# An attention and mixture-of-experts layer on one core: unread products, another order of the row products and earlier projections in its opening

## The chip, the cores and the metric

The kernel runs on one NeuronCore of a Trainium2 chip. A core has TensorE (PE: matrix products into PSUM, with weight loads, PEld, beside them), VectorE (DVE), ScalarE (ACT), GpSimd (POOL) and SyncE (SP), which mainly issues DMAs; each works through its own instructions in order. The metric is the time of one execution on the device in microseconds, and lower is better. A profiled execution also leaves a trace, whose span runs from the first to the last instruction.

## The reference, cut to what matters

The input x is 8 sequences of 1024 tokens of 256 numbers. Attention has 16 heads of 16; keys and values are the same rotated projection. Then 8 experts each take the 1024 tokens that score highest for them.

```python
x = x + attn(layernorm(x), Wq, Wkv, Wout, bout)
x = x + moe(layernorm(x), gate_w, ln_w, ln_b, fc1s, b1s, fc2s, b2s)

def attn(x, ...):
    q, kv = split(x @ Wq), split(x @ Wkv)            # 16 heads of 16
    q, kv = rotary(q) * 16 ** -0.5, rotary(kv)
    out = softmax(q @ kv.T) @ kv
    return merge(out) @ Wout + bout

def moe(x, ...):                                      # x: 8192 tokens
    scores = softmax(x @ gate_w.T)
    w, idx = top_k(scores.T, 1024)                    # for each of 8 experts
    y = layernorm(x[idx]) * ln_w + ln_b
    out = (gelu(y @ fc1.T + b1) @ fc2.T + b2) * w
    return x.at[idx].add(out)
```

## The kernel before

**Tiling and stages.** All tiles have 128 rows. Attention goes batch by batch (8) and, in a batch, over 4 groups of 4 heads. A group has 16 steps: for the row maxima a step is one tile of 128 queries against half of the keys; for the exponentials it is 128 keys against half of the queries. The maxima run 13 steps ahead of the exponentials (`LEAD`), so the main loop starts at step -13, and the first exponentials come at step 0. Then the experts' tokens are selected, gathered and put through the two layers.

**Numbers in two halves.** [...] So q, k and the differences of neighbouring keys ("steps", tile `s`) are cut into a high half `hi` and the rest `lo`, and one product over 64 rows (16 dimensions times four combinations of halves) gives an exact score. `split_halves` makes hi and lo for q and k, `split_steps` (L361) for the key differences (`dhi`, `dlo`). The halves are written to DRAM (`q_d`, `k_d`, `s_d`) in the laid-out order and loaded back as `q`, `k` and `s`. For the first heads the trip through DRAM would take long, so `rows_at_once` (L164) lays hi and lo out on TensorE: a product with `picks` copies rows of hi and lo to their places, two pairs of heads beside each other, and ACT or DVE copies the result into the `q` and `k` tiles.

**A step.** `row_max` makes a score product `ps_x` (L536), which VectorE reduces to a row maximum (L543); there are four in a step. `score_pass` makes `ps_s` (L587) from `s` and `q` with a last product that takes the maximum away (from the tile `top`, which `lay_max` sends through DRAM, L573 and L577), ACT takes the exponential (L620), and `weigh_values` multiplies with the values (`ps_av`, L639).

**PSUM.** `ps_m` has four buffers of one bank and serves nearly everything: `ps_x`, transposes `ps_t`, `ps_av`. `ps_e` has two of two banks, for `ps_s`, the row products `ps_r`, and the projections `ps_p` of heads 8 to 15 in the first batch. A buffer can be written again once its last reader is done.

**What sets the order.** The order on each engine is the order in which the program emits instructions. The rest of the work is cut into pieces by generators: each `yield` ends a piece and names its kind ("x" is heavy and comes one to a step, in step -1 and before in every step, later in every second). `run_pieces` advances up to two of the tasks in `starts` by one piece, after the step's own score products. The first of them is `prologue(0)`: it normalises and turns x, projects heads 0 to 7 (`c` = 0), rotates them (`rotate`, on VectorE at first, later on POOL), transposes and splits them with four calls of `rows_at_once`, and goes on with heads 8 to 15 (`c` = 1): 8 projections, one for each tile of 128 tokens (L292), then four transposes with their splits. Up to the point where `ready[0, 0]` is set the pieces are run at once, before step -13; the last `rows_at_once` comes in step -13, the two `split_steps` of heads 0 to 7 in steps -12 and -11, and the projections in steps -10 to -3. Writes wait in `pending` until `issue_pending` hands them to SP, whose queue then holds in order: the writes of q and k, the loads of the next group's k and q, the late weights, the writes of `s_d`, the loads of `s`.

Of the kernel before, what the change touches and what calls it, by code (L numbers as in the profile page):

```python
# [8 lines left out]
F32 = mybir.dt.float32  # L9
# [10 lines left out]
P = 128  # L20
H = 16
DH = 16
# [5 lines left out]
def preln_attention_moe_kernel(  # L28
# [18 lines left out]
    nc = tc.nc  # L47
# [11 lines left out]
    QW = 512  # L59
# [18 lines left out]
    same = const.tile([P, P], F16, name="same")  # L78
# [19 lines left out]
    with ExitStack() as actx:  # L98
# [62 lines left out]
        picks = prob.tile([P, 4, P], F32R, tag="e", name="picks")  # L161
        nc.gpsimd.tensor_copy(picks, picks_f)

        def rows_at_once(hi, lo, keys, dst, eng):  # L164

            pt = ps_e.tile([P, 2, QW], F32, tag="e", name="ps_r")
            for pair in range(2):
                dims = slice(2 * DH * pair, 2 * DH * (pair + 1))
                for part, half in enumerate((hi, lo)):
                    nc.tensor.matmul(  # L170
                        pt[:, pair],
                        lhsT=picks[dims, 2 * keys + part],
                        rhs=half[dims],
                        start=(part == 0),
                        stop=(part == 1),
                    )
            if eng is nc.scalar:
                nc.scalar.copy(dst, pt)
            else:
                nc.vector.tensor_copy(dst, pt)  # L180
# [102 lines left out]
        def project(b, t, xnT, qk, c, n):  # L283

            if b == 0 and c > 0:

                pp = ps_e.tile([P, 2, QW], F32, tag="e", name="ps_p")[:, 0, 0 : 2 * n * P]
            else:
                pp = ps_m.tile([P, QW], F32, tag="m", name="ps_p")[:, 0 : 2 * n * P]
            for kc in range(DC):  # L290
                w = wqkv[:, kc, :, c * P : (c + n) * P]
                nc.tensor.matmul(  # L292
                    pp,
                    lhsT=xnT[:, kc, t % T2 * P : (t % T2 + 1) * P],
                    rhs=w.rearrange("p a d -> p (a d)") if n == DC else w,
                    start=(kc == 0),
                    stop=(kc == DC - 1),
                )
            rotate(b, t, pp, qk, c, n)
# [4 lines left out]
        def issue_pending():  # L304
            while pending:
                fn, *args = pending.pop(0)
                fn(*args)
# [53 lines left out]
        def split_steps(b, hf, c, full):  # L361


            dif = side.tile([P, QW], F32, tag="u", name="dif")
            if hf == 0:
                nc.gpsimd.tensor_copy(dif[:, 0:P], full[:, 0:P])
                tails[0] = small.tile([P, P], F32, tag="tail", name="tail", bufs=1)
                nc.gpsimd.tensor_copy(tails[0], full[:, QW - P : QW])
            else:
                nc.gpsimd.tensor_tensor(dif[:, 0:P], full[:, 0:P], tails[0], ALU.subtract)  # L370
            nc.gpsimd.tensor_tensor(dif[:, P:QW], full[:, P:QW], full[:, 0 : QW - P], ALU.subtract)
            hi = side.tile([P, QW], F32R, tag="hi", name="dhi")
            lo = side.tile([P, QW], F32R, tag="lo", name="dlo")
            (nc.scalar.copy if b == 0 and c == 0 else nc.gpsimd.tensor_copy)(hi, dif)
            nc.gpsimd.tensor_tensor(lo, dif, hi.bitcast(F32), ALU.subtract)
            rows, cols = slice(c * P, (c + 1) * P), slice(hf * QW, (hf + 1) * QW)
            pending.append((write_halves, halves[b][2], rows, cols, hi, lo, True))
            if hf == 1:
                pending.append((steps_ready.setdefault, (b, c), True))
# [8 lines left out]
        def prologue(b):  # L388

            q_d = dram.tile([2, D, 4, QW], F32, tag="q_d", name=f"q_d{b}", bufs=2)  # L390
            k_d = dram.tile([D, 4, N], F32, tag="k_d", name=f"k_d{b}", bufs=2)
            s_d = dram.tile([D, 4, N], F32, tag="s_d", name=f"s_d{b}", bufs=2)
            halves[b] = (q_d, k_d, s_d)
            if b == 0:
                k = kq.tile([P, 2, N], F32R, tag="k", name="k_0", bufs=2)
                grp[0] = {
                    "k": k,
                    "q": [
                        kq.tile([P, 2, QW], F32R, tag="q", name=f"q_0_{hf}", bufs=4)
                        for hf in range(2)  # L400
                    ],
                }
                xts = [xt_first, load_x(b, 1)]
            else:
                xts = [load_x(b, hf) for hf in range(2)]
                yield 6 if b == 1 else 2
            qks = []

            def normalised(hf):
                stats = yield from row_stats(xts[hf], "a", 2 if b == 0 else 1)  # L410
                scaled(nc.vector if b == 0 else nc.gpsimd, xts[hf], xts[hf], stats)

            def turned(hf):

                tag = "aoT" if b == 0 and hf == 1 else "T"
                xnT = one.tile([P, DC, QW], F32, tag=tag, name=f"xnT_{b}_{hf}")
                for c in range(DC):
                    pt = transposed(lambda t: xts[hf][:, t, c * P : (c + 1) * P])
                    nc.scalar.copy(xnT[:, c, :], pt)
                qks.append(side.tile([P, T2, 2, D], F32, tag="qk", name=f"qk_{b}_{hf}"))  # L420
                return xnT

            if b == 0:

                xnTs = []
                yield from normalised(0)
                yield "x"
                xnTs.append(turned(0))
                yield from normalised(1)
                for hf in range(2):  # L430
                    if hf == 1:
                        yield "x"
                        xnTs.append(turned(1))
                    for j in range(T2):
                        yield "x"
                        project(b, T2 * hf + j, xnTs[hf], qks[hf][:, j], 0, 1)
            else:
                yield from normalised(0)
                yield from normalised(1)
                yield 3  # L440
                for hf in range(2):
                    yield "x"
                    xnT = turned(hf)
                    if hf == 0:


                        yield (2 * T * NG * (b - 1) - 5,)
                    for j in range(T2):
                        yield "x"
                        project(b, T2 * hf + j, xnT, qks[hf][:, j], 0, DC)  # L450
            for c in range(DC):
                fulls = []
                if b == 0 and c > 0:
                    for t in range(T):
                        yield "x"
                        project(b, t, xnTs[t // T2], qks[t // T2][:, t % T2], c, 1)
                if b == 0 and c == 0:

                    for n, (hf, s) in enumerate(((0, 0), (0, 1), (1, 1), (1, 0))):
                        yield "x"  # L460
                        pt = transposed(lambda j: qks[hf][:, j, s, 0:P])
                        full = split_halves(b, hf, c, s, pt)
                        if s == 1:
                            fulls.append((full, pt))
                        issue_pending()
                        if n > 0:
                            rows_at_once(*at_once.pop(0))
                    for n, (full, pt) in enumerate(fulls):
                        nc.scalar.copy(full, pt)
                        fulls[n] = full  # L470
                    ready[b, c] = True

                    yield "s"
                    rows_at_once(*at_once.pop(0))
                else:
                    for hf in range(2):
                        for s in range(2):
                            yield "x"
                            issue_pending()
                            pt = transposed(lambda j: qks[hf][:, j, s, c * P : (c + 1) * P])  # L480
                            full = split_halves(b, hf, c, s, pt)
                        yield 2
                        issue_pending()
                        split_steps(b, hf, c, full)
                if b == 0 and c == 0:
                    for hf in range(2):
                        yield "s"
                        split_steps(b, hf, c, fulls[hf])
                        issue_pending()
            yield 2  # L490
            issue_pending()

# [989 lines left out]
```

## Time and profile before

| | |
|---|---|
| median of 3 runs | 2214.38 us (2210.72 to 2216.36) |
| profiled execution | 2207.54 us |
| span of its trace | 2205.8 us |
| mean granted TensorE clock | 0.978 of full |
| PE busy over the span | 2056.1 us (93%) |
| DVE busy over the span | 1765.4 us (80%) |
| opening, to the first row maximum | 29.6 us |
| step 0, first product for exponentials | 61.6 us |

Lines of the profile give a start and a length in microseconds, the engine, the line of the kernel, the operation, output and inputs by the program's names, and the count of instructions that a row sums up. A bracket at the end says how long the engine had been idle before and what ended the wait. "Busy" counts an instruction from its start to its end; products overlap, so a row of eight is shorter than eight single ones.

### The profile page before, as it was taken

Reading aid. Unit: us, or ns where it says so; the run is one execution under the profiler, and the core shown is the slowest. Engines: PE = TensorE matmul, PEld = TensorE weight load, DVE = VectorE, ACT = ScalarE, POOL = GpSimd, SP = SyncE. Lnnn points to the kernel's source line nnn. Section 1 sums busy time; section 2 is a strip of 40 time slices with the busy share of each in tenths; the row PEclk is TensorE's granted clock in tenths of the full one; section 3 lists DMA queues with packets and bytes.
Section 4 is the critical chain, followed back from the end, with each engine's and each line's share of the span. In section 5 each row is a group of like instructions: output and inputs, shape, how many; then the busy total and the mean of one; then the engine's idle time right before and its main releaser. Section 6 shows DMA issues by size and latency. Waiting matters only on the chain.

```text
span 2205.8 us, 35134 instructions
## 1 busy us (share of the span) xinstructions
PE 2056.1 (93%) x12528; PEld 1100.0 (50%) x12528; DVE 1765.4 (80%) x3446; ACT 1384.7 (63%) x1791; POOL 1272.5 (58%) x1320
## 2 busy tenths in 40 slices
PE   7999999999999999999999999999993599999998
PEld 4444544444444444444444444444431376666665
DVE  8988888998998899889989988989946646666654
ACT  2777777777887777878777877877781112222222
POOL 6667585848485766758584867644242144444442
PEclk9999999999999999999999999999996699999999
DMA  6523624632372356236323722552114033333322
GB/s 178 191 88 123 238 81 147 223 122 78 136 257 73 104 202 206 96 107 225 143 78 143 270 67 102 188 208 88 41 41 135 20 75 75 77 77 77 76 42 24
DMA packets 152703, 271.53 MB, mean 123 GB/s; under 512 B 15056, under 2 KB 67664, under 8 KB 152400
## 3 DMA queue, kind: packets, MB, share of 16 engines
q1 hardware_dynamic: 139088, 250.62, 32.9%
q0 software_dynamic: 12288, 17.05, 4.7%
q8 instruction: 99, 1.62, 0.3%
q10 hardware_dynamic: 1152, 1.62, 0.2%
q14 instruction: 76, 0.62, 0.1%
HBM read 143.93 MB, written 125.04 MB: 122 GB/s over the span
## 4 chain that ended last, share of the span: by engine, by line
PE 71%; DVE 16%; issue 4%; POOL 3%; ACT 2%; DMA 2%; POOLq 0%; ACTq 0%; SPq 0%; DVEq 0%
PE ps_av L639 20%; DVE mx L543 14%; PE ps_x L536 13%; PE ps_o L1333 10%; PE ps L1279 8%; PE ps_s L587 7%; PE ps_p L292 5%; PE ps_t L251 3%; PE ps_o L727 3%; PE ps_h L1238 1%; POOL xf L242 1%; ACT e L620 1%; PE ps_d L665 1%; DVE xr L735 1%; PE ps_y L1194 1%
## 5 line engine op out<-in xcount | busy, mean ns | idle before, releaser
L543 DVE TENSOR_REDUCE mx<-ps_x 128x1 f32<-128x512 f32 x2048 | 1264.1, 681 | 153.1 <-PE ps_x L536 139.8
L620 ACT ACTIVATE e<-ps_s 128x1024 f32<-128x1024 f32 x1024 | 995.4, 1025 | 88.6 <-PE ps_x L536 42.1
L536 PE MATMUL ps_x<-k,q 64*128 64x512 f32 x2048 | 718.9, 449 | 19.7 <-DVE mx L543 6.2
L587 PE MATMUL ps_s<-q,s 64*128 64x512 f32 x2048 | 622.2, 428 | 9.0 <-ACT e L620 6.1
L536 PEld LDWEIGHTS ps_x<-k,q 64*128 64x128 f32 x2048 | 347.4, 185 | 414.1 <-DVE mx L543 287.8
L639 PE MATMUL ps_av<-e,v 128*32 128x512 f32 x4096 | 492.5, 598 | 6.9 <-DVE mx L543 0.9
L654 POOL TENSOR_TENSOR av<-av,avp 128x512 f32<-128x512 f32 x190 | 242.4, 1276 | 396.4 <-ACT avp L652 380.2
L587 PEld LDWEIGHTS ps_s<-q,s 64*128 64x128 f32 x2048 | 314.0, 185 | 46.9 <-ACT e L620 29.6
L1333 PE MATMUL ps_o<-w,hT 128*128 128x256 f32 x1024 | 230.2, 381 | 0.0
L639 PEld LDWEIGHTS ps_av<-e,v 128*32 128x32 f32 x4096 | 107.0, 109 | 241.7 <-issue 163.6
L1343 POOL DMA_INDIRECT out<-o,idx x64 | 103.0, 1609 | 212.9 <-DVE o L1342 80.2
L1333 PEld LDWEIGHTS ps_o<-w,hT 128*128 128x128 f32 x1024 | 191.8, 190 | 29.3 <-issue 4.8
L652 ACT COPY avp<-ps_av 128x512 f32<-128x512 f32 x192 | 112.8, 587 | 144.4 <-PE ps_av L639 139.9
L1231 ACT ACTIVATE hT<-mid,b 128x512 f32<-128x512 f32 x112 | 77.9, 719 | 98.9 <-DVE mid L1306 73.9
L1291 ACT COPY mid<-ps 128x512 f32<-128x512 f32 x28 | 16.0, 571 | 195.7 <-PE ps L1279 195.7
L292 PE MATMUL ps_p<-wqkv,xnT 128*128 128x512 f32 (+1 forms) x288 | 129.8, 578 | 4.5 <-DVE mx L543 4.1
L1341 DVE TENSOR_TENSOR o<-ps_o,b2b 128x256 f32<-128x256 f32 x64 | 27.1, 423 | 128.8 <-PE ps_o L1333 126.2
L269 POOL TENSOR_TENSOR u<-pe,sin 128x256 f32<-128x256 f32 (+1 forms) x128 | 86.2, 695 | 53.8 <-ACT pe L263 53.8
L1179 POOL DMA_INDIRECT g<-rows_d,idx x64 | 63.9, 998 | 92.1 <-issue 68.0
L339 POOL CAST hi<-full 128x512 fp32r<-128x512 f32 x60 | 36.9, 615 | 89.8 <-ACT full L337 80.7
L273 POOL TENSOR_TENSOR qk<-pe,u 128x512 f32<-128x512 f32 (+1 forms) x72 | 83.3, 1157 | 7.2 <-DVE pe L271 2.2
L340 POOL TENSOR_TENSOR lo<-full,hi 128x512 fp32r<-128x512 f32 x60 | 76.9, 1281 | 7.5 <-DMA s_d<-dlo 2.9
(200 smaller groups left out, 2323.8 us busy)
## 6 DMA issues: line engine op xcount, KB each, us to landing
s<-s_d SPq DMA_DIRECT2D x64, 512.0 KB
k<-k_d SPq DMA_DIRECT2D x62, 512.0 KB
q<-q_d SPq DMA_DIRECT2D x124, 256.0 KB
s_d<-dhi SPq DMA_DIRECT2D x32, 512.0 KB
s_d<-dlo SPq DMA_DIRECT2D x32, 512.0 KB
w<-in_fc_t SPq DMA_DIRECT2D x16, 1024.0 KB
q_d<-hi SPq DMA_DIRECT2D x30, 512.0 KB
q_d<-lo SPq DMA_DIRECT2D x30, 512.0 KB
```

Source lines behind the costliest of these rows:

```text
L269: eng.tensor_tensor(u[:, :, a * hd : (a + 1) * hd], v4[:, :, 1 - a, :], s3, ALU.mult)
L292: nc.tensor.matmul(pp, lhsT=xnT[:, kc, t % T2 * P : (t % T2 + 1) * P], rhs=w.rearrange("p a d -> p (a d)") if n == DC else w, start=(kc == 0),
L536: nc.tensor.matmul(pt, lhsT=q[r : r + 64, h // 2, j * P : (j + 1) * P], rhs=k[r : r + 64, h // 2, kh * QW : (kh + 1) * QW], start=True, st ...
L543: nc.vector.tensor_reduce(grp[i]["mx"][:, kh, h, j : j + 1], pt, AX.X, ALU.max)
L587: nc.tensor.matmul(pt[:, h % 2, :], lhsT=ones_r[r : r + 64, :] if last else k[r : r + 64, pair, kt * P : (kt + 1) * P], rhs=(top_bufs[half ...
L620: nc.scalar.activation(e.rearrange("p h q -> p (h q)"), pt.rearrange("p h q -> p (h q)"), AF.Exp, scale=DH**-0.5,)
L639: nc.tensor.matmul(pa[HS * h : HS * (h + 1), :], lhsT=v_bufs[b % 2][:, kt, c : c + HS], rhs=es[h // 2][:, h % 2, :], start=(n == 0), stop= ...
L652: nc.scalar.copy(part, pa)
L654: (nc.vector if end else nc.gpsimd).tensor_tensor(av, av, part, ALU.add)
L1279: nc.tensor.matmul(ph, lhsT=lhsT, rhs=rhs, start=True, stop=True)
L1333: nc.tensor.matmul(po, lhsT=h[:, f, j * P : (j + 1) * P], rhs=weights[e][1][:, f, :], start=(n == 0), stop=(n == FC - 1),)
L1343: nc.gpsimd.indirect_dma_start(out=out_rows[:, :], out_offset=bass.IndirectOffsetOnAxis(ap=idx[:, t : t + 1], axis=0), in_=o, in_offset=No ...
```

## The change

A helper `busy(n)` emits n products of the 128x128 matrix `same` with itself, read four times over, into a `ps_m` buffer that nobody reads. `rows_at_once` takes the high halves of both pairs first and then both low halves, with one such product ahead of each; it is called four times. Two more stand after the point where `ready[0, 0]` is set. The two `split_steps` of heads 0 to 7 lose their own pieces and go into those of the first two projections of heads 8 to 15, so that the projections begin in step -12 rather than -10, and everything that `prologue(0)` does after them comes two steps sooner.

```diff
+        def busy(n):
+
+            for _ in range(n):
+                pb = ps_m.tile([P, QW], F32, tag="m", name="ps_b")
+                nc.tensor.matmul(
+                    pb.rearrange("p (a q) -> p a q", a=4),
+                    lhsT=same,
+                    rhs=same.unsqueeze(1).to_broadcast([P, 4, P]),
+                    start=True,
+                    stop=True,
+                )
+
         def rows_at_once(hi, lo, keys, dst, eng):
 
             pt = ps_e.tile([P, 2, QW], F32, tag="e", name="ps_r")
-            for pair in range(2):
-                dims = slice(2 * DH * pair, 2 * DH * (pair + 1))
-                for part, half in enumerate((hi, lo)):
+            for part, half in enumerate((hi, lo)):
+                busy(1)
+                for pair in range(2):
+                    dims = slice(2 * DH * pair, 2 * DH * (pair + 1))
                     nc.tensor.matmul(
                         pt[:, pair],
                         lhsT=picks[dims, 2 * keys + part],
                         rhs=half[dims],
...
                 if b == 0 and c > 0:
                     for t in range(T):
                         yield "x"
+                        if t < 2:
+                            split_steps(b, t, 0, first_fulls[t])
+                            issue_pending()
                         project(b, t, xnTs[t // T2], qks[t // T2][:, t % T2], c, 1)
...
                     ready[b, c] = True
+                    busy(2)
 
                     yield "s"
                     rows_at_once(*at_once.pop(0))
...
                 if b == 0 and c == 0:
-                    for hf in range(2):
-                        yield "s"
-                        split_steps(b, hf, c, fulls[hf])
-                        issue_pending()
+                    first_fulls = fulls
             yield 2
             issue_pending()
```

## The prediction

> **What bounds the kernel now.** I read the page first: how busy each engine is, and the TensorE clock over the span.
>
> ```profile
> PE 2056.1 (93%) x12528; PEld 1100.0 (50%) x12528; DVE 1765.4 (80%) x3446; ACT 1384.7 (63%) x1791; POOL 1272.5 (58%) x1320
> PE   7999999999999999999999999999993599999998
> PEclk9999999999999999999999999999996699999999
> ```
>
> TensorE bounds the whole, but a slice is 55 us wide and the edit lives in the first 70. So I asked for windows of the opening, cut where the granted clock changes.
>
> ```profile
> 24.86:28.28 3.42, 3.33 (x18) 1.91 (x19) 1.66 (x3) 2.09 (x3) 1.00 (x3) 1.00 0.80 174
> 28.28:31.69 3.41, 2.80 (x13) 1.18 (x11) 3.41 (x6) 2.12 (x4) 1.41 (x3) 1.00 0.92 199
> 31.69:35.10 3.41, 3.41 (x8) 1.46 (x6) 3.41 (x7) 1.40 (x2) 2.00 (x4) 0.51 0.93 204
> 35.10:38.52 3.42, 3.42 (x7) 1.90 (x7) 3.42 (x6) 0.62 (x1) 1.97 (x2) 0.50 0.85 258
> 38.52:41.95 3.43, 3.43 (x10) 1.86 (x10) 2.21 (x5) 0.37 (x1) 1.59 (x3) 0.50 1.01 353
> 58.90:62.30 3.40, 3.04 (x17) 1.63 (x15) 3.40 (x7) 1.18 (x3) 3.15 (x6) 1.00 0.25 71
> ```
>
> Columns: length, busy time and count of PE, weight loads, DVE, ACT, POOL, then clock, DMA share, GB/s. From 31.7 to 42.0 us TensorE runs at half clock. But from 28.3 on the full column is DVE's: 3.41 of 3.41, except in one window (2.21). VectorE's own timeline says what that exception is.
>
> ```profile
> 28.94 0.68 DVE L333 TENSOR_TENSOR lo<-ps_t,hi 128x512 fp32r<-128x512 f32 x1
> 29.61 9.68 DVE L543 TENSOR_REDUCE mx<-ps_x 128x1 f32<-128x512 f32 x16
> 40.50 9.74 DVE L543 TENSOR_REDUCE mx<-ps_x 128x1 f32<-128x512 f32 x16 [1.22 <-PE ps_x L536]
> ```
>
> The row maxima run back to back at 9.68/16 = 0.605 us each; between 29.6 and 62 us VectorE waits once, 1.22 us, for TensorE. It stays at 47.2 of 48.4 us to 110 us, and only then TensorE takes over (88.0 of 90 us). So a microsecond here is worth one at the end only if it moves the VectorE row of maxima: its start (29.61), or its one hole.
>
> TensorE's timeline gives both.
>
> ```profile
> 25.56 0.66 PE L251 MATMUL ps_t<-ident,qk 128*128 128x128 f32 x4
> 26.15 0.74 PE L170 MATMUL ps_r<-kl,picks 32*128 32x512 f32 x4
> 26.82 0.66 PE L251 MATMUL ps_t<-ident,qk 128*128 128x128 f32 x4
> 27.40 1.28 PE L170 MATMUL ps_r<-kl,picks 32*128 32x512 f32 x4
> 29.08 1.77 PE L536 MATMUL ps_x<-k,q 64*128 64x512 f32 x4 [0.40 <-DVE k L180]
> ...
> 37.67 2.07 PE L292 MATMUL ps_p<-wqkv,xnT 128*128 128x256 f32 x4
> 43.47 1.13 PE L292 MATMUL ps_p<-wqkv,xnT 128*128 128x256 f32 x4
> ```
>
> The first score product waits for the copy of k (VectorE, 27.81 to 29.02). The hole is the first projection at half clock: 2.07 us against 1.13. VectorE had at most four products in PSUM, 4 x 0.605 = 2.4 us; the projection plus the next product's 0.6 us is more.
>
> **The change, part by part.** *Unread products.* Ten: two in each of four `rows_at_once`, two before step -13. The experts' opening has the same product:
>
> ```profile
> 1740.39 1.90 PE L1088 MATMUL ps_b<-ones_h,same 128*128 128x512 f16 x8
> ```
>
> One alone takes 0.38 us at full clock, so seven steps take 1.90 - 0.38: 0.217 us each, 2.2 us in all. Nobody reads them; they cost where TensorE had no gap. Those of the first call go into waits for hi (23.76 to 24.00) and lo (24.5 to 24.9). From 25.56 on TensorE is nearly full. Summing starts: transposes 25.56 + 0.59; k's first rows 0.67 + two products 0.43, so the next transposes stand at 27.25, k's second rows at 27.84. There product, hi, product bring the lo pair to about 28.5 (its lo is ready at 27.89, no wait now) and its end to 28.75; two more give 29.2 against 29.08: +0.1 us. If each also pays its weight load (0.10 us in the experts' rows), six make +0.7. A buffer can add as much: the four PSUM buffers of that pool are held here by transposes awaiting later readers, and a product put into the last one waits for lo (end 29.62), so scores start near 29.85, +0.75. Below nothing: 0.1 us, through hi pairs now side by side. I take +0.4 us, between the sum of starts and the ends, range -0.1 to +0.75.
>
> *High before low.* Same products, same durations; both hi products of a call can go before lo arrives. It is counted in the -0.1.
>
> *The clock.* [...] I go by the trace: clock held, hole gone, -1.22 us. Ends: 0 and -1.22.
>
> *Projections two steps sooner.* Two empty stops vanish; both `split_steps` stay at steps -12 and -11, now each ahead of a projection, and all later work for heads 8 to 15 moves two steps (4.8 us) up. On TensorE 8 projections x 1.13 = 9.0 us stand in steps that VectorE fills with 2.42 us against 0.9 + 1.13 of TensorE: hidden. If the dip comes all the same, they help: the first projection goes out after the eighth score product, 32.4 to 34.5, the window to 35.1 is then as full as the one that ended the dip, and the hole is about 0.6 instead of 1.22.
>
> POOL: a projection costs it 0.87 + 0.73 + 0.73 + 0.29, every 2.79 us by its starts (43.01, 45.80, 48.60), more than a step. The second `split_steps` now queues behind the first rotation: POOL is done with the first dlo at 34.4, rotates to 37.2 (37.6 at half clock), differences 1.5, ACT's copy 0.6, dlo 1.3: 40.7 to 41.1 instead of 37.8. Who waits is SP:
>
> ```profile
> 42.71 1.19 SPq L315 DMA_DIRECT2D s_d<-dlo  x1
> ```
>
> ```profile
> 58.36 1.49 SPq L577 DMA_DIRECT2D top<-top_d x2
> 61.93 0.62 PE L587 MATMUL ps_s<-top,ones_r 64*128 64x512 f32 x2
> ```
>
> SP reaches that write only at 42.7, behind the loads of k, q and the late weights, so 1.6 us of cover remain; gone, each further microsecond delays s, then top_d, which queues behind s. The top load issued at 58.36 won't come sooner, while its product would be due at 61.1; a wait there of up to 0.8 us is hidden, because VectorE is then still 1.1 us behind (max 53 starts at 29.61 + 52 x 0.605 + 1.22 + 0.42 = 62.7). PE's backpressure through two copies and two PSUM tiles reaches four projections back: the eighth, at 50, needs the fourth rotation, done at 49. Cover 1 us, price 0.4 us a projection. SP's writes for heads 8 to 15 come after the top loads in its order and find DMA at 0.25: 0. ACT issues the same copies: 0. After step 9 every queue's order is as before.
>
> **Sum**: +0.4 - 1.22 + 0 = -0.8 us. The profiled execution took 2207.54 us (span 2205.8), so 2206.7; it lies 6.8 below the runs' median 2214.38, to which I apply the same difference: **2213.6 us**.
>
> **Rivals.** (a) *It does not do what it says*: the dip comes all the same. +0.4 - 0.6 = -0.2, at worst with a buffer wait +0.75 - 0: **2214.2 to 2215.1**. [...] (b) *Faster by more*. The chain that ended last has places where it waits for DMA:
>
> ```profile
> 216.99 4.90 DMA q<-q_d
> ```
>
> There the second batch's queries come late, and near 437 the score products wait 2.1 us for top. If the shifted opening lets both transfers win, -0.8 - 4.8 - 2.1 = -7.7: **2206.7**. For it: such waits stand at some batch boundaries and not at others (none at 640, 1030). Against: the order after step 9 is unchanged, so issue and need shift together. (c) *Slower*: the late dlo. If POOL's rotation holds the second dlo past 42.7 + 1.6 us of slack at top, about 44.3, every microsecond more delays the exponentials of step 0 and, with TensorE in order, the maxima. From 51.7 on it outweighs the 0.8 by 6.6; at 52.8 it is 8.5 - 0.8 = 7.7: **2222**. It needs over ten microseconds beyond my 41, for instance through ACT's in-order copies waiting on POOL. (d) A boundary stall added, the opposite of (b): +4.9 or so, **2219**.
>
> **How the numbers follow.** Forecast 0.5; (a) 0.24; (b) 0.11; (c) 0.09; (d) 0.06. A difference within 0.3%, 6.6 us, is about what a measurement of this kernel can tell from no change (three runs of it span 5.6 us). Forecast, (a) and half of (d) are within it: same 0.77; faster 0.11; slower 0.12. The range: forecast to (d), plus the runs' own 2.8 us to either side, cut where (b) and (c) begin: 2209 to 2219.
>
> **What the changed profile would show.** Right: clock 1.00 from 31.7 to 42; the maxima start at 29.9 to 30.3 with no hole to step 0; first projection of heads 8 to 15 near 33; s_d<-dlo still issued near 42.7. Wrong: a first score product later than 30.4; a hole of a microsecond with clock 0.5; SP waiting for POOL dlo; top late with VectorE idle; or all this as said and the end elsewhere, at the DMA waits of the batch boundaries.

## The result: slower by 0.19%

| | before | changed |
|---|---|---|
| median | 2213.22 us (12 runs) | 2216.7 us (12 runs) |
| ratio, 95% interval | 1 | 1.0019 (1.001 to 1.0028) |
| span of the profiled execution | 2205.8 us | 2213.2 us |
| mean granted TensorE clock | 0.978 | 0.977 |

The change costs 4.2 us, 2.2 to 6.2 by the interval, where 0.8 us of gain was forecast. The page of the changed kernel (busy time of each engine, and the clock over 40 slices of the span) looks as before.

```profile
PE 2060.6 (93%) x12538; PEld 1101.1 (50%) x12538; DVE 1767.1 (80%) x3446; ACT 1384.2 (63%) x1791; POOL 1270.5 (57%) x1320
PEclk9999999999999999999999999999996699999999
```

The ten products more are there, and no slice of 55 us shows a difference. The windows of the opening do (length, busy time and count of PE, PEld, DVE, ACT, POOL, clock, DMA share, GB/s).

```profile
28.28:31.69 3.41, 3.07 (x11) 1.08 (x11) 2.21 (x4) 2.30 (x4) 0.72 (x3) 1.00 0.92 198
31.69:35.10 3.41, 3.41 (x12) 1.25 (x11) 1.78 (x4) 1.11 (x2) 0.76 (x1) 0.60 0.93 204
35.10:38.52 3.42, 3.42 (x9) 1.94 (x10) 2.74 (x6) 0.79 (x2) 2.13 (x3) 0.50 0.87 277
38.52:41.95 3.43, 3.43 (x14) 1.91 (x13) 3.43 (x7) 0.14 (x1) 3.11 (x5) 0.90 0.97 337
```

VectorE, which was full here in every window but one, is busy 2.21, 1.78 and 2.74. TensorE looks fuller, yet its clock still goes to half, at 32.3 instead of 31.7, and comes back at 39.1 instead of 42.0. VectorE's timeline names the holes.

```profile
28.70 0.68 DVE L346 TENSOR_TENSOR lo<-ps_t,hi 128x512 fp32r<-128x512 f32 x1
30.59 2.49 DVE L557 TENSOR_REDUCE mx<-ps_x 128x1 f32<-128x512 f32 x4 [1.20 <-PE ps_x L550]
34.70 2.48 DVE L557 TENSOR_REDUCE mx<-ps_x 128x1 f32<-128x512 f32 x4 [1.63 <-PE ps_x L550]
37.86 14.44 DVE L557 TENSOR_REDUCE mx<-ps_x 128x1 f32<-128x512 f32 x24 [0.68 <-PE ps_x L550]
...
55.69 16.97 DVE L557 TENSOR_REDUCE mx<-ps_x 128x1 f32<-128x512 f32 x28 [0.46 <-PE ps_x L550]
```

Before, the maxima started at 29.61 and had one hole of 1.22. Now they start 0.98 later, and the holes are 1.63, 0.68 and 0.46. Sum: 0.98 + 2.77 - 1.22 = +2.5 us; the rest lies in waits too short for the rows to name. As a mark I use the start of the second layout of the maxima (the row `parts<-mx`), called the opening's end: 69.94 before, 72.70 now, +2.76. TensorE's timeline shows what stands in front of the maxima.

```profile
25.32 0.66 PE L264 MATMUL ps_t<-ident,qk 128*128 128x128 f32 x4
25.82 0.38 PE L168 MATMUL ps_b<-same 128*128 128x512 f16 x1
26.12 0.50 PE L183 MATMUL ps_r<-kl,picks 32*128 32x512 f32 x2
26.56 0.39 PE L168 MATMUL ps_b<-same 128*128 128x512 f16 x1
26.88 0.50 PE L183 MATMUL ps_r<-kl,picks 32*128 32x512 f32 x2
27.31 0.65 PE L264 MATMUL ps_t<-ident,qk 128*128 128x128 f32 x4
...
29.30 0.82 PE L168 MATMUL ps_b<-same 128*128 128x512 f16 x2
30.05 0.62 PE L550 MATMUL ps_x<-k,q 64*128 64x512 f32 x2
...
32.61 0.61 PE L168 MATMUL ps_b<-same 128*128 128x512 f16 x1
33.15 0.79 PE L183 MATMUL ps_r<-lo,picks 32*128 32x512 f32 x2
33.87 1.22 PE L550 MATMUL ps_x<-k,q 64*128 64x512 f32 x4
...
55.16 0.73 PE L550 MATMUL ps_x<-k,q 64*128 64x512 f32 x4 [0.51 <-ACT mrows L585]
```

The first score product goes out at 30.05 instead of 29.08, behind the products. The last row products and their two unread ones (31.77 to 33.87) stand between the scores of steps -13 and -12 and meet the half clock: that is the hole of 1.63. The score products at 55.16 wait for ACT's copy of the row maxima (`mrows`): that is the hole of 0.46.

### The profile page after: what moved, and what is told of

Read it like the earlier page. It is cut to its first block, busy times and chain, and to the rows that moved or that the text cites. A ratio compares the mean times of both kernels' runs of the same rounds, so it can differ in the third digit from the quotient of the medians.

```text
span 2213.2 us, 35158 instructions
## 1 busy us (share of the span) xinstructions
PE 2060.6 (93%) x12538; PEld 1101.1 (50%) x12538; DVE 1767.1 (80%) x3446; ACT 1384.2 (63%) x1791; POOL 1270.5 (57%) x1320
## 4 chain that ended last, share of the span: by engine, by line
PE 71%; DVE 16%; issue 4%; POOL 4%; DMA 3%; ACT 2%; SPq 0%; POOLq 0%; ACTq 0%; DVEq 0%
PE ps_av L653 20%; DVE mx L557 14%; PE ps_x L550 12%; PE ps_o L1347 10%; PE ps L1293 8%; PE ps_s L601 7%; PE ps_p L305 5%; PE ps_t L264 3%; PE ps_o L741 3%; PE ps_h L1252 1%; POOL xf L255 1%; ACT e L634 1%; PE ps_d L679 1%; DMA top_d<-mrows 1%; DVE xr L749 1%
## 5 line engine op out<-in xcount | busy, mean ns | idle before, releaser
L1347 PEld LDWEIGHTS ps_o<-w,hT 128*128 128x128 f32 x1024 | 191.8, 190 | 29.3 <-issue 4.8
L1193 POOL DMA_INDIRECT g<-rows_d,idx x64 | 63.7, 995 | 98.6 <-issue 68.1
```

What stands on the lines that cost most here:

```text
L1347: nc.tensor.matmul(po, lhsT=h[:, f, j * P : (j + 1) * P], rhs=weights[e][1][:, f, :], start=(n == 0), stop=(n == FC - 1),)
```

## The experiments

Three theories: the **products** cost, on a TensorE that has no gap; the **move** costs, through ACT and POOL; or the loss is made at the **batch boundaries**, where transfers win or lose. Each ratio is against runs of the kernel before from the same session. "Half clock" says where the granted clock was 0.50, found in windows of 0.2 us; "end" is the opening's end; all these times are of one profiled execution.

| kernel | ratio (95% interval) | first maximum | end | half clock |
|---|---|---|---|---|
| before | 1 | 29.61 | 69.94 | 31.7-42.0 |
| changed | 1.0019 (1.0010-1.0028) | 30.59 | 72.70 | 32.3-39.1, 63.1-66.5 |
| e1 | 1.0007 (0.9999-1.0016) | 29.75 | 71.52 | 30.1-36.9, 57.5-67.7 |
| e2 | 1.0033 (1.0023-1.0043) | 32.50 | 75.57 | 34.9-48.7, 72.5-75.9 |
| e3 | 1.0011 (1.0000-1.0021) | 29.87 | 72.42 | 29.9-36.7, 53.9-67.5 |
| e4 | 0.9995 (0.9985-1.0006) | 29.39 | 69.90 | 31.3-41.5 |
| e5 | 1.0016 (1.0006-1.0025) | 30.57 | 73.23 | 27.3-37.5, 57.9-71.5 |
| e6 | 1.0031 (1.0020-1.0043) | 31.23 | 73.85 | 34.1-37.5, 58.1-71.7 |
| e7 | 1.0000 (0.9988-1.0011) | 29.38 | 69.84 | 31.3-41.5 |
| e8 | 1.0028 (1.0019-1.0038) | 29.44 | 74.13 | 29.5-43.1, 63.7-70.5 |
| e9 | 1.0037 (1.0024-1.0050) | 29.82 | 71.82 | 29.3-36.1 |
| e10 | 1.0015 (1.0005-1.0025) | 29.39 | 72.19 | 31.5-38.3, 58.7-65.5, 68.9-72.3 |
| e11 | 1.0028 (1.0018-1.0038) | 30.57 | 73.15 | 31.7-45.3 |
| e12 | 1.0025 (1.0015-1.0035) | 29.60 | 74.81 | 31.5-34.9, 55.5-69.1 |
| before again | | 29.61 | 70.06 | 31.5-41.7 |
| changed again | | 30.57 | 72.59 | 32.5-39.3, 63.1-66.5 |

Four of these executions started late. The copy of k begins at 27.95 in e1 and 28.24 in e6 (27.57 in the changed kernel), and at 28.06 in e3 and 28.41 in e5 (27.81 before). The input was there at 10.76 as in the others, but the first 16 projections, from 12.88 on, took 5.49, 5.79, 5.38 and 5.73 us in these four, against 4.60 before and 4.89 in the changed kernel. So 0.25 to 0.67 us of their ends are not their edits', and where their clock falls can't be laid to their edits either. In all executions with more than one fall, the falls lie a whole number of 3.40 to 3.43 us apart (changed: 32.3 and 63.1, nine times 3.42). Divided by 3.42, the times of the first falls leave remainders of 0.5 to 3.4 us, within 0.2 of each other in the two profiles of one kernel; what places them is not shown.

The mark also has limits. Set against the second profile of before, e2 and e10 lose a further 1.3 us between it and the next layout of the maxima. e9 is the slowest of all in time although its end is only 1.88 us later; no trace here explains that.

**e1: the changed kernel without the ten products.**

```diff
             for part, half in enumerate((hi, lo)):
-                busy(1)
                 for pair in range(2):
...
                     ready[b, c] = True
-                    busy(2)
```

> The changed kernel without its ten unread products; the order of the row products and the earlier projections stay. If the products on a full TensorE cause the loss, the first row maximum starts near 29.4 us (29.61 before, 30.59 after), the opening's end (the second layout of the row maxima, 69.94 before, 72.70 after) comes at 69.5 to 70.5, and the time is within 0.1% of before. If the earlier projections cause it, the opening still ends near 72 and the time is 0.1% or more above before. If the loss is made at the transfers of the batch boundaries, the opening tells nothing and the time stays above before although it ends near 70.

The time fell to 1.0007, within 0.1% of before as the products theory had it; the end, 71.52, lay between the two values expected. Its VectorE timeline:

```profile
29.75 2.54 DVE L555 TENSOR_REDUCE mx<-ps_x 128x1 f32<-128x512 f32 x4
33.19 2.48 DVE L555 TENSOR_REDUCE mx<-ps_x 128x1 f32<-128x512 f32 x4 [0.91 <-PE ps_x L548]
36.35 14.44 DVE L555 TENSOR_REDUCE mx<-ps_x 128x1 f32<-128x512 f32 x24 [0.67 <-PE ps_x L548]
```

The late start is gone, and the hole at the last row products is 0.91 although the clock fell 2 us sooner. 0.67 and a later 0.45 stay; e3, which has the move alone, has the 0.67 too, and waits of the same kind in place of the 0.45.

**e2: the ten products alone, in the old order.**

```diff
             for pair in range(2):
                 dims = slice(2 * DH * pair, 2 * DH * (pair + 1))
+                busy(1)
                 for part, half in enumerate((hi, lo)):
...
                     ready[b, c] = True
+                    busy(2)
```

> The kernel before with the ten unread products alone (one ahead of each pair of heads, since the old order goes by pairs). If the products cause the loss: first row maximum near 30.6, a hole at the last row products in half clock, end of the opening at 71.5 to 72.5, time 0.1 to 0.2% above before. If the earlier projections cause it: start 29.6 to 30, end of the opening at 69.5 to 70.3, time as before.

Worse than the products theory said: first maximum 32.50, end +5.6, time +0.33%.

```profile
26.82 0.38 PE L168 MATMUL ps_b<-same 128*128 128x512 f16 x1
27.13 0.73 PE L183 MATMUL ps_r<-kl,picks 32*128 32x512 f32 x2
27.80 0.39 PE L168 MATMUL ps_b<-same 128*128 128x512 f16 x1
```

In the old order the two row products behind an unread one are hi and lo of one pair, on the same rows: from 27.13 to 27.80, 0.67 us. In the changed kernel they belong to two pairs: from 26.12 to 26.56, 0.44. Over the four such places of k that is 0.9 us. The rest comes from the first call, which waits for lo with its second pair still to do: the transposes behind it start at 26.33, not 25.32. And with projections as late as before, the first half clock lasts 13.8 us (34.9 to 48.7), against 6.8 in the changed kernel.

**e3: the earlier projections alone.**

```diff
                     for t in range(T):
                         yield "x"
+                        if t < 2:
+                            split_steps(b, t, 0, first_fulls[t])
+                            issue_pending()
                         project(...)
...
-                    for hf in range(2):
-                        yield "s"
-                        split_steps(b, hf, c, fulls[hf])
-                        issue_pending()
+                    first_fulls = fulls
```

> The kernel before with the projections of heads 8 to 15 two steps sooner, nothing else. Products theory: the first row maximum stays at 29.6, the hole of 1.22 us shrinks to about 0.6 or splits in two, and the opening ends at 69.3 to 70.3. If the earlier projections cause the loss: POOL, loaded with both, makes ACT's copies and the copy of the row maxima late, holes of 0.4 us or more near 53 to 60, end of the opening at 71 or later.

The products theory missed here: end 72.42, and in this execution the move alone costs about 2.2 us once the late start is taken off. The hole did split (0.67 and 0.67), but new ones come:

```profile
54.56 2.48 DVE L543 TENSOR_REDUCE mx<-ps_x 128x1 f32<-128x512 f32 x4 [0.72 <-PE ps_x L536]
57.25 2.63 DVE L543 TENSOR_REDUCE mx<-ps_x 128x1 f32<-128x512 f32 x4 [0.20 <-PE ps_x L536]
60.19 12.20 DVE L543 TENSOR_REDUCE mx<-ps_x 128x1 f32<-128x512 f32 x20 [0.31 <-PE ps_x L536]
```

The waits of ACT and of PE in the same kernel (who waited for whom: us in total, times, longest) say whose:

```profile
ACT pe L263 <- POOL qk L273: 12.8, 5, 3.3
PE ps_x L536 <- ACT mrows L571: 0.5, 1, 0.5
```

ACT's copies of the projections wait for POOL's rotations, the copy of the maxima waits behind them in ACT's order, and TensorE's next score product waits for its buffer.

**e4: high halves before low ones, alone.**

```diff
-            for pair in range(2):
-                dims = slice(2 * DH * pair, 2 * DH * (pair + 1))
-                for part, half in enumerate((hi, lo)):
+            for part, half in enumerate((hi, lo)):
+                for pair in range(2):
+                    dims = slice(2 * DH * pair, 2 * DH * (pair + 1))
```

> The kernel before with high halves ahead of low ones, nothing else. All theories: first row maximum 0.0 to 0.25 us sooner, because the first copy of q starts sooner, the opening ends at 69.6 to 70.0, time as before.

As expected: maxima 0.22 us sooner, given back in a hole of 0.18, no measurable difference. Its TensorE timeline is the scale for one product:

```profile
25.33 0.66 PE L251 MATMUL ps_t<-ident,qk 128*128 128x128 f32 x4
25.92 0.73 PE L170 MATMUL ps_r<-kl,picks 32*128 32x512 f32 x4
26.58 0.66 PE L251 MATMUL ps_t<-ident,qk 128*128 128x128 f32 x4
```

From transposes to transposes 1.25 us; in the changed kernel, with two products between, 25.32 to 27.31 = 1.99. So **0.37 us each**, not 0.217.

**e5 and e6: e3 and the changed kernel, with ACT's copies in six buffers.**

```diff
-            pe = side.tile([P, 2 * D], F32, tag="pe", name="pe")[:, 0:W]
+            if b == 0 and c > 0:
+                pe = prob.tile([P, 2, QW], F32, tag="e", name="pe")[:, 0, 0:W]
+            else:
+                pe = side.tile([P, 2 * D], F32, tag="pe", name="pe")[:, 0:W]
```

> The kernel before with the earlier projections alone, and ACT's copies of these projections in a ring of six buffers instead of two, so that ACT need not wait for POOL. If the loss of the earlier projections (opening's end 72.42 with two buffers) comes from ACT waiting for POOL with TensorE and VectorE behind it, the holes in the row maxima between 51 and 62 (0.72, 0.20 and 0.31 us) vanish, step 0 stands a microsecond sooner, and the opening ends at 70.5 to 71.3. If it comes from the clock, which fell to half once more at 54, the holes stay or move, and the end stays near 72.

> The changed kernel with the same ring of six buffers. If ACT's wait is one part and the unread products the other: the row maxima still start near 30.6 and still have the hole of about 1.6 us at the last row products, the hole of 0.46 near 55 is gone, and the opening ends near 72.0 (72.70 with two buffers). If ACT's wait is all of it, the end comes near 70.

Both expectations were half right. In e6 the hole of 0.46 is gone and the late start stays, but the hole at the last row products is 0.82 (the clock fell only at 34.1), and the end is 73.85, not 72.0. e5's maxima run without a hole from 52.2 on, so the holes there were ACT's wait for POOL; but then:

```profile
52.17 15.21 DVE L546 TENSOR_REDUCE mx<-ps_x 128x1 f32<-128x512 f32 x25
68.03 1.89 DVE L546 TENSOR_REDUCE mx<-ps_x 128x1 f32<-128x512 f32 x3 [0.65 <-PE ps_x L539]
70.71 2.48 DVE L546 TENSOR_REDUCE mx<-ps_x 128x1 f32<-128x512 f32 x4 [0.79 <-PE ps_x L539]
```

The holes had moved to step 0, which ran at half clock (57.9 to 71.5); e6 has the same two, 0.64 and 0.80. The ring brought a cost of its own: ACT's table load for the exponentials, at 60.07 in e3, comes at 64.40 in e5, in step 0. I had not foreseen it, so neither run prices the ring.

**e7: two products, only where TensorE waits** (with e4's order).

```diff
+        fills = [1, 1]
...
             for part, half in enumerate((hi, lo)):
+                if fills:
+                    busy(fills.pop())
```

> The kernel before with high halves ahead of low ones and only two of the ten unread products, those of the first call of the row products, where TensorE waits. If a product costs only where TensorE has no gap: as the order alone, first row maximum 29.4, end of the opening 69.9, time as before. If the products disturb in another way (buffers, weight loads of the next product), the first row maximum is 0.2 us or more later than with the order alone.

First maximum 29.38 against e4's 29.39, end 69.84 against 69.90, ratio 1.0000: there the products cost nothing that shows.

**e8: nine products in steps -13 to -11** (with e4's order).

```diff
                     rows_at_once(*at_once.pop(0))
+                    busy(3)
...
+            if s == -LEAD + 1 or s == -LEAD + 2:
+                busy(3)
             run_pieces(s, ...)
```

> The kernel before with high halves ahead of low ones, and nine unread products elsewhere: three after the row products of step -13 and three after the scores of each of steps -12 and -11, where TensorE waits for VectorE. If enough wide work holds the clock: no half clock between 30 and 42, no hole of 1.22 us at the first projection, end of the opening 68.6 to 69.0. If the clock falls all the same, the products take 0.43 us each at half clock and the steps become longer than VectorE's 2.42: end of the opening 71 or later.

The clock had fallen at 29.5, before the first of them, and at half clock they stretched the steps: holes of 2.06, 0.88 and 0.88, end 74.13. It tells what late products cost, not whether the clock could be held.

**e9: e5 and four products in each of steps -2 and -1. e12: the same on e3.**

```diff
+            if s in (-2, -1):
+                busy(4)
             run_pieces(s, ...)
```

> The kernel before with the earlier projections, the ring of six copies, and four unread products of 128 rows after the scores of each of steps -2 and -1, from which the move took the transposes. If those two steps, left with products of 64 rows alone, let the clock fall just ahead of step 0: no half clock between 50 and 75, no holes of 0.4 us or more after 62, and the opening ends at 71.0 to 72.0 (73.23 without them, in an execution whose first maxima also started 0.6 us late). If the second fall has another cause, it comes again and the end stays at 73 or later.

> The kernel before with the earlier projections (the old ring of two copies) and four unread products of 128 rows after the scores of each of steps -2 and -1. If the second fall of the clock, ahead of step 0, is what the thin steps cost: no half clock from 50 to 75, the holes near 53 to 56 stay, those after 57 go, and the opening ends at 71.2 to 71.9 (72.42 without the products). If the fall is harmless: end 72.3 or later.

In e9 the second fall is gone and the end is 71.82, as expected; one hole of 0.59 is more than I allowed, in the step that now holds the table load. Its row of products also gives their price beside each other:

```profile
59.12 1.46 PE L168 MATMUL ps_b<-same 128*128 128x512 f16 x4
```

At full clock, in a row of their own kind, they follow each other every (1.46 - 0.38) / 3 = 0.36 us.

In e12 the expectation failed: the clock fell at 55.5, ahead of the products, whose rows of four then take 2.3 us, and the end is 74.81 against 72.42 in e3.

```profile
60.27 2.32 PE L168 MATMUL ps_b<-same 128*128 128x512 f16 x4
62.52 1.35 PE L548 MATMUL ps_x<-k,q 64*128 64x512 f32 x4
64.09 2.30 PE L168 MATMUL ps_b<-same 128*128 128x512 f16 x4 [0.23 <-DVE mx L555]
```

So the empty steps are not the only reason. In e1, e3, e5 and e6 too the second fall (53.9 to 58.1) comes before the scores of step -2, the first of the two steps (58.55 in e5). Had the clock fallen in e9 where it did in e5, at 57.9, the products at 59.12 would have come too late. That they held the clock in e9 is therefore not shown.

**e10: order, earlier projections, six copies, transposes in their old steps.**

```diff
                         project(...)
+                    for _ in range(2):
+                        yield "s"
```

> High halves ahead of low ones, the projections two steps sooner, the ring of six copies, but the transposes and all after them in their old steps (two empty stops behind the projections); no unread products. If the earlier projections themselves are harmless and only what left steps -2 and -1 and ACT's wait cost: no half clock between 45 and 75, a first hole of 0.6 to 1.3 us in all, end of the opening 69.3 to 70.3, time as before. If earlier projections cost by themselves: end at 71 or later.

Missed: the clock fell at 58.7, after the two steps that are empty now, -4 and -3, and once more at 68.9. Ending the projections two steps sooner leaves two steps with score products alone, wherever they are put.

**e11: products and order, without the move.**

```diff
-                        if t < 2:
-                            split_steps(b, t, 0, first_fulls[t])
-                            issue_pending()
...
-                    first_fulls = fulls
+                    for hf in range(2):
+                        yield "s"
+                        split_steps(b, hf, c, fulls[hf])
+                        issue_pending()
```

> The changed kernel without its earlier projections: the ten unread products with the new order of the row products. If products and move each cost on their own and add up (changed kernel +2.7 at the opening's end, order alone 0, move alone about +2.2): first row maximum 30.6, end of the opening 70.5 to 71.0 (+0.6 to +1.1). If the products cost the same whatever the order (+5.6 with the old order): 73 or later. If the products cost nothing without the move: 69.9 to 70.2.

Products and move don't add up: without the move the opening ends later still, +3.2 (the ratio, 1.0028, is not told from the changed kernel's 1.0019 by their intervals).

```profile
30.57 2.48 DVE L557 TENSOR_REDUCE mx<-ps_x 128x1 f32<-128x512 f32 x4 [1.19 <-PE ps_x L550]
35.11 7.27 DVE L557 TENSOR_REDUCE mx<-ps_x 128x1 f32<-128x512 f32 x12 [2.05 <-PE ps_x L550]
43.59 9.86 DVE L557 TENSOR_REDUCE mx<-ps_x 128x1 f32<-128x512 f32 x16 [1.22 <-PE ps_x L550]
```

The products give the late start and the hole of 2.05; the 1.22 of before stays. The earlier projections end the half clock sooner (39.1 against 45.3) and so take off part of what the products cost.

**Both kernels once more.**

> The kernel before, unchanged. If the gaps that open between two profiles at the batch boundaries (near 220 to 245 and 425 to 450 us) are chance, this profile differs from the first one of the same kernel there by one to several microseconds, with the opening ending at 69.7 to 70.3 in both. If they follow from the opening, the two agree at every boundary.

> The changed kernel, unchanged. If its loss in the opening is the kernel's own: first row maximum 30.4 to 31.3, half clock once between 31 and 40 and once more near step 0, end of the opening 72.2 to 73.9. If it was one execution's clock, some of this is missing.

The columns are four layouts of the maxima (`parts<-mx`), named by their time in the first profile of before, and the span.

| behind the first profile of before by, us | end of opening | 245.8 | 448.0 | 1619.4 | span |
|---|---|---|---|---|---|
| before again | 0.12 | 2.41 | 5.09 | 5.69 | 4.1 |
| e4 (order alone) | -0.04 | 1.55 | 4.82 | 5.09 | 3.7 |
| changed | 2.76 | 3.90 | 6.11 | 7.48 | 7.4 |
| changed again | 2.65 | 3.56 | 6.67 | 8.68 | 10.6 |

The opening repeats to 0.12 us. At the boundaries near 220 to 245 and 425 to 450 the unchanged kernel falls behind itself by 2.3 and 2.7 us; e4, not slower in time, does the like. The first profile of before was a lucky one there. The boundary theory falls as a cause of the opening's loss; the boundaries are the noise on top of it. Against the second profile of before, the changed kernel is 2.6 us behind at the end of the opening, still 2.7 at 217 us, and 1.5, 1.0 and 1.8 at the later marks, so how much of the opening's loss reaches the end has to be taken from the many runs, not from a profile.

## Why the prediction was wrong

The measured 2216.7 lies inside the stated range, 2209 to 2219, but only because the range is wide: the sum that led to 2213.6 failed in two of its terms.

**The bound** was right: the losses in the opening came out as a later start or a hole in VectorE's maxima.

**The unread products, "+0.4 us".** The bracket was exceeded. I summed them at 0.217 us each, the step of a row in the experts' opening, and called that the same product. It is not: that row reads `ones_h`, 512 columns, where `busy` reads `same` four times over (`ps_b<-ones_h,same` against `ps_b<-same`). The one that was added takes 0.37, and 0.36 in a row of its own (e9). Six of them at 0.15 more put 0.9 on the 0.1 of my sum of starts; measured is +0.98 in the start, or +1.20 against the order alone. The wait for a buffer, which I had put at up to 0.75, is not needed for it. And I priced the calls of k, but not the two products in the last call, between the scores of steps -13 and -12, which met the half clock: with them the hole there is 1.63. Start and hole, 2.6 us, are the loss at the opening's end.

**"Clock held, hole gone, -1.22".** This step failed outright, and no run shows its term. The clock fell in every one of the sixteen profiled executions, with all ten products at 31.7 to 34.9, against 31.7 and 31.5 in the two profiles of before; how much of that delay is theirs is not shown. That wide products (on 128 rows) hold the clock was my estimate from two windows of before: 28.28 to 31.69, with products on 32 and 64 rows, 2.80 of 3.41 us busy and the fall behind it, and 58.90 to 62.30, with transposes on 128 rows, 3.04 of 3.40 busy and the clock full. The first fall in the changed kernel came with TensorE busy 3.06 of the 3.40 us ahead of it (28.90 to 32.30), and nine of the ten wide products issued by then. And width alone does not explain the traces: these two windows, of before and of the changed kernel, hold products of 64 rows (`ps_x`, `ps_s`) and nothing wider.

```profile
62.47:65.89 3.42, 2.46 (x15) 1.32 (x16) 3.42 (x7) 3.41 (x4) 3.26 (x5) 1.00 1.06 383
63.07:66.48 3.41, 3.33 (x14) 2.32 (x14) 3.41 (x7) 1.02 (x1) 3.25 (x5) 0.50 1.04 378
```

The clock stayed full through the first and behind it; at the end of the second it came back from half. They hold 15 and 14 products, the window ahead of the second fall (59.65 to 63.07) 7, which may count, but wasn't tested. What does decide is open. A hole of 0.68 stands where 1.22 was, near the 0.6 priced as the fallback, and the dip lasts 6.8 us instead of 10.3; that the shorter dip made the hole smaller is not shown (both holes lie at half clock, and e10, with the move as well, has 1.10 and 0.57).

**"Cover 1 us, price 0.4 us a projection" and "ACT issues the same copies: 0".** The cover was not there: the second dlo came at 42.5 to 43.8, not 41, since ACT's first dhi stood behind the late copy of q (33.99), and the rotations ran 3 us behind my table. What waited was not a projection but ACT's copy of the maxima, 0.46 us. In the prediction I had named this queue only as a way to a late dlo. Nor had I asked what is left in steps -2 and -1 when their transposes go: a second stretch of half clock ahead of step 0 (63.1 to 66.5). In the changed kernel it was harmless to the maxima, which run through it without a hole (the row of 28 from 55.69 to 72.66); in e5 and e6 the longer stretch (57.9 to 71.5) held two.

**Rivals.** (a), that the dip comes all the same, is the one that happened in its first half; its worst case, +0.75, left out the products at half clock and ACT's wait. The late write of dlo (c) did not bind: SP issued it at 43.81, a microsecond later than before, and top was in time. (b) and (d), stalls at the boundaries, can't be told from the boundaries' own noise.

**What stays open.** The opening explains 2.7 of 4.2 us; the rest is inside the interval, and I can't tell it from the boundaries' noise. What decides when the clock falls is not known. Whether enough products could hold the clock at no cost was not shown: e8 started too late for that.

No version beats the kernel before: the order alone (0.9995, 0.9985 to 1.0006) is not told from it.

## What to carry to other kernels

Here filling an engine's waits was free where the wait outlasted the filler (e7, end 69.84 against e4's 69.90), and not where the engine had no gap: set each filler between the two instructions it parts, at the price measured for that very product (here 0.37 us, not the 0.217 of one with another operand), and drop those that fall where the engine is full. Before work is moved to earlier steps, ask what the steps it leaves still hold, since here the clock fell at 63.1 behind 3.4 us of score products alone, and walk through the in-order queue of each engine that serves the moved work, not only the one that bounds.

## What the runs showed of the hardware that was not expected

- The clock fell while TensorE looked busy: 3.06 of the 3.40 us ahead of the first fall in the changed kernel (28.90 to 32.30), 3.05 of 3.40 in e11 (28.2 to 31.6). Score products alone (64 rows) filled the 3.4 us ahead of the second fall in the changed kernel (2.88 busy), but such products also stood in a window that kept the full clock (before, 62.47 to 65.89, 2.46 busy), and in e12 the clock fell at 55.5 with four transposes of 128 rows, from 54.43 on, in the 3.4 us ahead (1.91 of 3.40 busy). Neither busy time nor width alone sorts these windows.
- The half-clock stretches of the sixteen executions lasted 3.4, 6.8, 10.2 or 13.6 us within the 0.2 us of the table, multiples of 3.4.
- An unread product of `same` with itself took 0.37 us of TensorE between row products (changed kernel against e4) and 0.36 in a row of its own kind (e9), where the experts' product of `same` with `ones_h` took 0.217 (before). Two row products with the step to the next unread one took 0.67 us on the same rows (e2) and 0.44 on different ones (changed kernel). What sets these was not tested. Operand and PSUM pool differ between the two unread ones; the weights alone don't tell them apart, since the experts' row loads `same` for each of its eight products too (1740.38, eight loads in 1.41 us).
